# A planned attention and expert kernel: the planner gets another model of the DMA queue and new ranks, a third buffer for the probabilities, and a second load of one expert's weights

## The chip, the core and the metric

The kernel runs on one core of one Trainium2 chip. The metric is device time in microseconds (us). TensorE is PE in the profile (its weight loads are PEld), VectorE is DVE, ScalarE is ACT, GpSimd is POOL. SyncE's queue (SPq) issues every DMA of this kernel.

## What is computed

There are 8 batches of 512 tokens of 256 features, a context of 512 x 512 per batch, and a mask over the context. First cross attention with 8 heads of 32, then a layer with a shared expert and 16 routed experts:

```python
    x = x + _L0_xattn_ref(ctx_2048, _layernorm(x, axis=-1), mask_BxS2_fk1, mask_BxS2_fk1, W_src, b_src, W_tgt, b_tgt, W_out, b_out)
    x = x + _L0_ffn_ref(_layernorm(x, axis=-1), gate_w, w_gate, w_up, w_down, sw_gate, sw_up, sw_down)
```

Attention projects the context to keys and values and the normalised x to queries, masks them, takes a softmax over 512 context positions per head, multiplies by the values, and projects [tgt, update] with W_out. The second layer normalises x again, computes 16 gate scores per token, keeps the top 8 as weights, and adds the weighted sum of all 16 experts (silu(x Wg) * (x Wu)) Wd (H = 128) to a shared expert of the same form.

## The kernel before

**Split numbers.** Each float32 operand of a large matmul is held as two float16 tiles, high part and rest, and each product is three matmuls (`mm3`, line 461).

**A recorded program, then a plan.** `record` (line 433) writes down every operation as an `Op` with its engine, a modelled duration in ns and its buffers. `schedule` (line 340) then plays these operations through a model of the five queues and fixes the order in which each engine gets them; the kernel issues them in that order, all from line 1071, which is why the profile shows one line. Engines run in order, so an instruction that waits holds all behind it. Among the operations that could start first the planner takes the one with the lowest due time, `vt`: a number in batches that `record` sets by hand, plus a correction from the table `RANK` (line 202) by kind of operation and stage (start, batch 0, batch 1, the last, the rest). `AHEAD` (line 201) says how far in due time an operation may run before the oldest one that is still open. `SLOTS` (line 30) gives the number of buffers of each pool; an operation that needs a buffer waits for a free slot.

**The DMA queue in the model.** A plain DMA (`dma`, line 197) takes 360 ns of SP's time, a transposing DMA of n tiles (`dmat`, line 194) takes max(1240, 16.4 n) ns. After that, line 413 lets a transfer start 900 ns later or when the one before it is done, and lasts size/250 ns, where a transposing DMA has size 4000 n.

**Start.** x, the attention weights and the context of batch 0 are loaded. The weights are scaled by powers of two (`spread` takes a maximum over partitions with two small matmuls, `ama` and `amb`; `power` makes the scale), transposed on PE (`wsT`, `wtT`, `woT`) and split. The context of batch 0 is masked on POOL, its row sums of squares (`junk`, ACT; then `csT` and `csB` on PE) give its scale, and it is turned on PE (`cT`); later batches are turned by DMA (`ch<-cn`). The 17 experts' raw weights (`raw`, pool W, three DMAs of 128 KB each) are squared (`sqw`, ACT or POOL) and summed (`fm`, PE) for their scale, and then turned into float16 pairs (`w`, pool W; one ACT and one DVE operation each).

**Attention of a batch.** Keys `k`, queries `q` and values `v`. Then eight units (4 groups u of head group and half, times 2 blocks of 128 tokens). One unit: `s` is 16 matmuls into the only four-bank PSUM buffer S; `nm` is the row maximum (DVE, 2.3 us); four exps `p` (ACT); then per pair of heads, two of them, a float16 copy `pn` (ACT) and its rest (POOL), a transposing DMA `pt<-pn` of 128 tiles, and 16 matmuls `o` with the values. The S buffer is free for the next unit after the four exps; a `pn` buffer after its `pt` landed. `oc` and `on` scale the result; after each half, `on` is turned by DMA (`oh<-om`; batch 0 by PE) and projected (`oo`), and the second layernorm follows: statistics, an inverse root with 13 small POOL operations (`r2h`, `r2t`), `xf`, the split `fm` and four DMAs `f<-fm`, then the gate logits `lg`.

**Experts.** For each expert matmuls `g` and `u` of the tokens, `a` (ACT tanh, DVE, POOL times the gate weight `cb`, which DMA spreads over the partitions), `u` times `a`, the split `h`, and after each group of 5, 4, 4, 4 experts the down projection `y`, added into x. The experts of batch b are worked on together with the attention of batch b+1; due times and `RANK` decide the mixture.

A unit is written below as batch, group, block: unit 2,1,0.

Of the kernel before, what the change touches and what calls it, by code (L numbers as in the profile page):

```python
# [200 lines left out]
AHEAD = 1.366  # L201
RANK = {
    "aACT": {0: 0.1537, 1: 0.0033, 2: -0.4983, 7: 0.1955},
    "aDVE": {0: 0.0254, 1: 0.2498, 2: -0.2428},
    "aPOOL": {0: -0.0113, 1: 0.6968, 2: 0.5586, 7: 0.0013},
    "amaPE": {-1: 0.2806},
    "ambPE": {-1: 0.1166},
    "bobDVE": {-1: 0.5078},
    "bobSP": {-1: -0.2061},
    "bvbDVE": {-1: 0.105},  # L210
    "cTPE": {0: 0.5508},
    "cbSP": {0: 0.2177, 2: 0.7056, 7: 0.5622},
    "cdSP": {0: 0.0041, 1: -0.029, 2: 0.2104},
    "chACT": {0: -0.6068},
    "chDVE": {0: 0.2153},
    "chSP": {1: 0.0075, 2: -0.8976, 7: -1.0876},
    "cnACT": {1: -0.6307, 2: -0.7293, 7: -0.9914},
    "cnDVE": {1: 0.0087, 2: -0.0023, 7: 0.0346},
    "colsSP": {-1: -0.0672},
    "csBPE": {2: -0.1535, 7: -0.0124},  # L220
    "csTPE": {0: -0.1204, 1: -0.0287, 2: -1.2814, 7: -0.0309},
    "ctACT": {0: 0.864, 1: 0.1003, 2: 0.7227, 7: -0.1018},
    "cxPOOL": {0: 0.6459},
    "cxSP": {-1: 0.0735, 1: 0.0526, 2: -0.9286, 7: -0.0609},
    "fACT": {0: 0.0039},
    "fDVE": {0: 1.0851},
    "fSP": {1: 0.3396, 2: -0.0242, 7: 0.4824},
    "fTPE": {0: 0.3035},
    "fmACT": {1: 0.3782, 2: -0.0974, 7: -0.0187},
    "fmDVE": {2: 0.5311, 7: -0.0959},  # L230
    "fmPE": {-1: -0.1267},
    "fmaPE": {-1: 0.1564},
    "fmbPE": {-1: -0.4319},
    "gPE": {0: 0.1235, 1: 0.207, 2: 0.1559, 7: 0.6056},
    "gTPE": {0: 0.3676, 1: 0.5965, 2: -0.1162, 7: -0.0034},
    "gsqDVE": {-1: -0.4317},
    "gw_nDVE": {-1: -0.1543},
    "gw_nSP": {-1: -2.0117},
    "gwsACT": {-1: 0.0234},
    "gwsDVE": {-1: 0.6316},  # L240
    "hACT": {0: -0.6213, 1: 0.3291, 2: -0.1853, 7: -0.0131},
    "hDVE": {0: 0.1408, 1: 0.0071, 2: -0.2515, 7: -0.0144},
    "hPOOL": {0: -0.3695, 1: 0.2141, 2: -0.0944, 7: 0.3346},
    "junkACT": {1: -0.0113, 2: -0.018, 7: 0.0007},
    "kACT": {0: 0.3565, 1: -0.9183, 2: -0.1216},
    "kDVE": {0: 0.4038, 1: 0.1818, 2: -0.0333, 7: 0.0991},
    "kPE": {0: -0.2174, 1: -0.0614, 2: -0.0344, 7: -1.3012},
    "lgPE": {0: 0.2761, 1: -0.3919, 2: -0.2135, 7: 0.0154},
    "mbSP": {-1: -0.7576, 1: 0.96, 2: 0.035, 7: 0.1462},
    "mcolDVE": {-1: -0.5544},  # L250
    "mkSP": {-1: -0.0456},
    "mkTPE": {-1: -0.2494},
    "mrDVE": {0: 0.88, 1: 0.1094, 2: 0.5668},
    "mvDVE": {0: 0.3115, 1: 0.2223, 2: 0.1576, 7: -0.6709},
    "mwDVE": {1: -0.5933, 2: 0.5831, 7: -0.1328},
    "nmACT": {0: 0.3158, 1: -0.251, 2: -0.0551, 7: -0.0427},
    "nmDVE": {0: 0.0026, 1: 0.0593, 2: -0.1259, 7: -0.1155},
    "oPE": {0: 0.0273, 1: -0.0232, 2: 0.0553, 7: 0.0423},
    "oTPE": {0: 0.1833},
    "ocACT": {0: 0.1024, 1: 0.1925, 2: 0.2005, 7: 0.4061},  # L260
    "ocDVE": {0: 0.1704, 1: -0.1219, 2: -0.6326, 7: -0.0917},
    "ohACT": {0: 0.4072},
    "ohDVE": {0: -0.1733},
    "ohSP": {1: 0.1129, 2: -0.0398, 7: -0.3174},
    "omACT": {2: 0.2922, 7: 0.0002},
    "omPOOL": {1: -0.0603, 2: -0.0508, 7: 0.7467},
    "onPOOL": {0: 0.7499, 1: -0.853, 2: -0.1829, 7: -0.2491},
    "onesPOOL": {-1: -0.3119},
    "ooPE": {0: 0.4931, 1: -0.4365, 2: -0.6844, 7: -0.4352},
    "outSP": {0: 0.4027, 1: -0.3028, 2: 0.4122, 7: 0.4538},  # L270
    "pACT": {0: 0.0182, 1: -0.6748, 2: -0.0234},
    "pnACT": {0: 0.2152, 1: 0.2561, 2: 0.1906, 7: 0.0196},
    "pnPOOL": {0: 0.1635, 1: 0.0141, 2: 0.2234},
    "ptSP": {0: 0.4655, 1: -0.4384, 2: 0.1266, 7: 0.3368},
    "qACT": {0: 0.1257, 1: -0.3375, 2: -0.3996, 7: -0.129},
    "qDVE": {0: -0.2704, 1: -0.4202, 2: -0.5367, 7: -0.2649},
    "qPE": {0: -0.3731, 1: -0.0506, 2: -0.194, 7: -1.1345},
    "qPOOL": {0: -0.0185, 1: 0.126, 7: -0.8731},
    "rDVE": {0: -0.1233, 1: -0.1058, 2: 0.0001, 7: -0.3334},
    "rawSP": {-1: -0.1474},  # L280
    "rhPOOL": {0: -0.1646, 1: -0.4627, 2: 0.6826, 7: 0.2987},
    "riDVE": {0: -0.198, 1: 0.6361, 2: 0.1284, 7: -0.0834},
    "sPE": {1: 0.0314, 2: -0.3686, 7: -0.8384},
    "scACT": {0: -0.0831, 1: 0.4518, 2: -0.1934, 7: -0.1498},
    "scDVE": {0: 0.3459, 1: -0.1583, 2: 0.1869, 7: -0.186},
    "scPOOL": {0: -0.0709, 1: 0.1093, 2: -0.1766, 7: 0.0205},
    "smallDVE": {-1: 0.3026, 1: -0.1537, 2: -0.254, 7: -0.5587},
    "smallPOOL": {-1: -0.2347, 0: -0.1282, 1: -0.3163, 2: 0.0089, 7: 0.0576},
    "sqwACT": {-1: -0.5218},
    "sqwPOOL": {-1: -0.1816},  # L290
    "tDVE": {0: 0.0006, 1: -0.5031, 2: 0.36, 7: 0.0922},
    "uDVE": {0: 0.1229, 1: 0.634, 2: -0.239, 7: -0.259},
    "uPE": {0: -0.1486, 1: 0.6035, 2: 0.715},
    "vACT": {0: 0.2058, 1: 0.1873, 2: -0.0086, 7: 0.1161},
    "vDVE": {0: 0.3577, 1: 0.1322, 2: -0.9791, 7: -0.0565},
    "vPE": {0: 1.1408, 1: -1.3367, 2: -0.1245, 7: 0.2457},
    "vPOOL": {0: -0.0824, 1: -0.3013, 2: -0.4353, 7: 0.59},
    "veDVE": {0: 0.124, 1: -0.0703, 2: -0.0253, 7: -1.3962},
    "vfDVE": {0: 0.0546, 1: -0.7051, 2: 0.0069, 7: 0.2438},
    "wACT": {-1: -0.1553},  # L300
    "wDVE": {-1: -0.0168},
    "wmaPE": {-1: -0.2382},
    "wmbPE": {-1: -0.7302},
    "woACT": {-1: -0.6539},
    "woDVE": {-1: 0.1164},
    "woTPE": {-1: 0.5609},
    "wo_nSP": {-1: 0.2082},
    "wsACT": {-1: -0.3273},
    "wsDVE": {-1: -0.0925},
    "wsTPE": {-1: 0.9299},  # L310
    "ws_naSP": {-1: -0.9149},
    "ws_nbSP": {-1: 0.0231},
    "wtACT": {-1: 0.4585},
    "wtDVE": {-1: 0.4299},
    "wtTPE": {-1: -0.4778},
    "wt_nSP": {-1: 0.0823},
    "xDVE": {0: 0.124, 1: 0.2257, 2: -0.3319, 7: 0.1379},
    "xPOOL": {0: -0.0121, 1: 0.02, 2: 0.1123, 7: -0.199},
    "xSP": {0: 1.1008, 1: 0.0058, 2: 0.0641, 7: 0.353},
    "xTPE": {0: 0.4516},  # L320
    "xfACT": {0: -0.1806, 1: 0.1451, 2: -0.1422, 7: -0.437},
    "xhDVE": {0: 0.6081},
    "xhSP": {1: 0.2024, 2: -0.7682, 7: 0.2589},
    "xmACT": {1: 0.1813, 2: 0.1954},
    "xmPOOL": {1: -0.0234, 2: 0.0256, 7: 0.0077},
    "xnACT": {0: 0.0363, 1: -0.1228, 2: 0.2161, 7: -0.0338},
    "xnSP": {-1: -4.4201, 1: -0.3353, 2: -0.0611, 7: -0.0009},
    "xoPE": {0: -0.2204, 1: -0.0378, 2: -0.3262, 7: -0.1335},
    "yPE": {0: 0.3541, 2: 0.148, 7: 0.1762},
# [772 lines left out]
```

## Time and profile before

| | us |
|---|---|
| median of 3 runs | 962.2 (960.25 to 963.15) |
| the profiled execution, its own time | 962.42 |
| its span on the core | 960.3 |
| PE busy (matmuls) | 860.6, 8007 instructions |
| DVE, ACT, POOL busy | 668.5, 654.2, 680.4 |
| DMA packets' time, share of 16 engines | 77.9% on the queue of all DMAs |
| mean granted TensorE clock | 0.972 |

Busy times of an engine do not overlap with themselves; what is missing to the span is the engine's idle time. Where an engine is the bound, its idle time is the price, and the list of waits says what ended it. The windows show busy us per engine between two moments, counted from the span's start, and behind each its number of instructions.

### The profile page before, as it was taken

Reading aid. Unit: us, or ns where it says so; the run is one execution under the profiler, and the core shown is the slowest. Engines: PE = TensorE matmul, PEld = TensorE weight load, DVE = VectorE, ACT = ScalarE, POOL = GpSimd, SP = SyncE. Lnnn points to the kernel's source line nnn. Section 1 sums busy time; section 2 is a strip of 40 time slices with the busy share of each in tenths; the row PEclk is TensorE's granted clock in tenths of the full one; section 3 lists DMA queues with packets and bytes.
Section 4 is the critical chain, followed back from the end, with each engine's and each line's share of the span. In section 5 each row is a group of like instructions: output and inputs, shape, how many; then the busy total and the mean of one; then the engine's idle time right before and its main releaser. Section 6 shows DMA issues by size and latency. Waiting matters only on the chain.

```text
span 960.3 us, 21139 instructions
## 1 busy us (share of the span) xinstructions
PE 860.6 (90%) x8007; PEld 547.0 (57%) x8007; DVE 668.5 (70%) x1311; ACT 654.2 (68%) x1133; POOL 680.4 (71%) x830
## 2 busy tenths in 40 slices
PE   3874768989789998989999999989999999999997
PEld 2452446766555565636655556646555666565655
DVE  6666778855876677757785688757886687567554
ACT  3588887874877687757786587757787777534231
POOL 4577778876768787677858786787848976853432
PEclk9886999999889999999999999999999999999999
DMA  8868787798699967999599977998499968951411
GB/s 254 271 124 175 138 157 130 151 197 162 121 205 184 201 133 139 211 191 178 104 198 182 197 145 137 204 191 181 88 189 197 178 110 144 214 120 26 123 56 44
DMA packets 395542, 152.43 MB, mean 159 GB/s; under 512 B 347008, under 2 KB 375216, under 8 KB 395440
## 3 DMA queue, kind: packets, MB, share of 16 engines
q1 hardware_dynamic: 395440, 151.08, 77.9%
q8 instruction: 63, 1.03, 0.5%
q14 instruction: 39, 0.32, 0.2%
HBM read 61.12 MB, written 4.46 MB: 68 GB/s over the span
## 4 chain that ended last, share of the span: by engine, by line
PE 55%; DMA 12%; ACT 11%; DVE 8%; POOL 5%; issue 3%; SPq 1%; POOLq 0%; ACTq 0%; DVEq 0%
PE y L1071 14%; PE u L1071 13%; PE g L1071 12%; DMA pt<-pn 8%; PE s L1071 4%; ACT p L1071 3%; PE o L1071 3%; POOL pn L1071 3%; PE v L1071 3%; DVE nm L1071 3%; PE k L1071 2%; ACT pn L1071 2%; DMA cb<-cd 2%; PE oo L1071 2%; SPq L1071 1%
## 5 line engine op out<-in xcount | busy, mean ns | idle before, releaser
L1071 POOL TENSOR_TENSOR pn<-p,pn 128x1024 f16<-128x1024 f32 x128 | 274.6, 2151 | 57.8 <-ACT pn L1071 48.7
L1071 PEld LDWEIGHTS <-w 128*128 128x128 f16 x1836 | 172.1, 98 | 172.1 <-issue 19.3
L1071 POOL TENSOR_TENSOR a<-a,cb 128x512 f32<-128x512 f32 (+1 forms) x144 | 166.1, 1165 | 73.5 <-DVE a L1071 34.6
L1071 ACT ACTIVATE p<-s,nm,small 128x512 f32<-128x512 f32 x256 | 192.3, 782 | 10.6 <-POOL pn L1071 8.1
L1071 PE MATMUL g<-f,w 128*128 128x512 f16 (+1 forms) x918 | 194.7, 357 | 3.7 <-DVE oc L1071 1.3
L1071 PE MATMUL u<-f,w 128*128 128x512 f16 (+1 forms) x918 | 194.1, 358 | 1.6 <-DVE a L1071 1.6
L1071 PE MATMUL y<-w,h 128*128 128x256 f16 x1632 | 185.9, 273 | 5.6 <-DVE h L1071 4.1
L1071 PEld LDWEIGHTS <-h 128*128 128x128 f16 x1632 | 158.5, 98 | 32.0 <-DVE h L1071 6.7
L1071 ACT CAST pn<-p 128x1024 f16<-128x1024 f32 x128 | 134.5, 1053 | 60.8 <-DMA pt<-pn 60.7
L1071 DVE TENSOR_REDUCE nm<-s 128x4 f32<-128x2048 f32 x64 | 146.2, 2285 | 14.7 <-PE s L1071 14.6
L1071 ACT ACTIVATE a<-g,small 128x512 f32<-128x512 f32 (+1 forms) x153 | 98.1, 645 | 51.7 <-PE g L1071 49.8
L1071 DVE SCALAR_TENSOR_TENSOR a<-a,g 128x512 f32<-128x512 f32 (+1 forms) x153 | 94.5, 622 | 39.1 <-ACT a L1071 38.0
L1071 ACT CAST h<-u 128x512 f16<-128x512 f32 (+1 forms) x117 | 62.8, 540 | 51.0 <-DVE u L1071 49.2
L1071 PEld LDWEIGHTS <-pt 128*128 128x128 f16 x2048 | 69.8, 97 | 36.8 <-DMA pt<-pn 16.5
L1071 DVE TENSOR_TENSOR h<-u,h 128x512 f16<-128x512 f32 (+1 forms) x117 | 72.6, 625 | 25.7 <-ACT h L1071 24.1
L1071 DVE SCALAR_TENSOR_TENSOR x<-y,small,x 128x512 f32<-128x512 f32 x64 | 47.8, 748 | 60.9 <-PE y L1071 60.6
L1071 DVE TENSOR_TENSOR u<-u,a 128x512 f32<-128x512 f32 (+1 forms) x108 | 68.4, 635 | 27.5 <-PE u L1071 22.7
L1071 PE MATMUL o<-v,pt 128*128 128x65 f16 (+1 forms) x2048 | 74.2, 187 | 13.5 <-DMA pt<-pn 10.9
L1071 PE MATMUL s<-k,q 32*128 32x512 f16 x768 | 56.1, 396 | 21.2 <-ACT p L1071 20.7
L1071 POOL TENSOR_TENSOR on<-oc,r 128x128 f32<-128x128 f32 x64 | 30.1, 472 | 31.9 <-DVE oc L1071 20.1
L1071 POOL TENSOR_TENSOR h<-a,h 128x512 f16<-128x512 f32 (+1 forms) x36 | 40.3, 1120 | 15.2 <-ACT h L1071 14.9
L1071 PE MATMUL k<-ch,ws 128*128 128x512 f16 x192 | 45.6, 390 | 5.4 <-DMA ch<-cn 4.1
(188 smaller groups left out, 1055.8 us busy)
## 6 DMA issues: line engine op xcount, KB each, us to landing
cb<-cd SPq DMA_DIRECT2D x112, 256.0 KB, 3.9
cx<-in_ctx_dram SPq DMA_DIRECT2D x32, 256.0 KB, 3.6
xn<-in_x_dram SPq DMA_DIRECT2D x16, 256.0 KB, 3.4
x<-in_x_dram SPq DMA_DIRECT2D x8, 512.0 KB, 4.3
cb<-cd SPq DMA_DIRECT2D x32, 128.0 KB, 3.5
out_dram<-x SPq DMA_DIRECT2D x16, 256.0 KB, 3.1
mb<-in_mask_BxS_fk_dram SPq DMA_DIRECT2D x8, 256.0 KB, 4.6
raw<-in_L_ffn_w_gate_dram SPq DMA_DIRECT2D x16, 128.0 KB, 3.3
```

The costliest lines, as they stand in the source:

```text
L1071: getattr(getattr(nc, eng), m)(*[real(v) for v in (*out, *args_)], **{k: real(v) for k, v in kw.items()})
```

## The change

The program that `record` writes is the same but for three more DMAs. What changes:

- The model of the DMA queue. A transposing DMA of n tiles now has size 6555 n at 272 bytes per ns, starts 650 - 4.7 n ns after its issue or when the queue is free, and holds SP until 900 ns before its end; a plain DMA starts 950 ns after its issue.
- `AHEAD` and all of `RANK`, so the order on every engine.
- Buffers: `pn` 2 to 3, `oc` 2 to 3, `act` 5 to 6; `row` 2 to 1, `oh` 2 to 1, `W` 18 to 17. `gsq` moves from pool `row` to pool `act`.
- The raw weights of the last expert (15) are loaded into a slot of pool `pn` instead of W, given up after the squares, and loaded again into a `pn` slot before their conversion.

```diff
-    x=2, n2=5, cx=4, c16=2, ch=1, xh=1, f=2, qk=4, row=2, mb=1, mx=2, mt=1, p32=2, pn=2, pp=3, v3=2, oc=2, oh=2,
-    cb=3, act=5, hx=6, W=NE + 1, cd=2, mr=1,
+    x=2, n2=5, cx=4, c16=2, ch=1, xh=1, f=2, qk=4, row=1, mb=1, mx=2, mt=1, p32=2, pn=3, pp=3, v3=2, oc=3, oh=1,
+    cb=3, act=6, hx=6, W=NE, cd=2, mr=1,
...
-    def add(self, eng, dur, calls, port=False, size=0, after=()):
+    def add(self, eng, dur, calls, port=False, size=0, after=(), lead=950.0):
...
+        op.lead = lead
...
     def dmat(self, tiles, out, in_):
-        self.add("SP", max(1240.0, 16.4 * tiles), [self.call("sync.dma_start_transpose", out, in_)], size=4000 * tiles)
+        self.add("SP", max(1240.0, 16.4 * tiles), [self.call("sync.dma_start_transpose", out, in_)], size=6555 * tiles, lead=650.0 - 4.7 * tiles)
...
-AHEAD = 1.366
+AHEAD = 1.37664868967
 RANK = {
-    "aACT": {0: 0.1537, 1: 0.0033, 2: -0.4983, 7: 0.1955},
...
+    "aACT": {0: -0.467, 1: -0.4329, 2: 0.0775},
...
         if e == "SP":
-            dma_free = max(dma_free, op.end + 900.0) + op.size / 250.0
+            dma_free = max(dma_free, st + op.lead) + op.size / 272.0
             op.end = dma_free
+            if op.lead < 950.0:
+                free[e] = max(free[e], dma_free - 900.0)
...
-    gsq = Buf("row", [P, D], F32, "gsq")
+    gsq = Buf("act", [P, D], F32, "gsq")
...
+    def load_raw(e, pool):
         sg, su, sd = (io["w_gate"][e], io["w_up"][e], io["w_down"][e]) if e < E else (io["sw_gate"], io["sw_up"], io["sw_down"])
-        raw = raws[e] = Buf("W", [P, 768], F32, f"raw{e}")
+        raw = Buf(pool, [P, 768], F32, f"raw{e}{pool}")
...
+        return raw
+
+    for n, e in enumerate(order):
+        p.vt = -1.9 + 0.001 * n
+        raw = raws[e] = load_raw(e, "W" if n + 1 < NE else "pn")
...
         raw = raws.pop(e)
+        if n + 1 == NE:
+            p.vt -= 0.1
+            raw = load_raw(e, "pn")
+            p.vt += 0.1
```

More of the change, by code (lines that the diff above doesn't have):

```diff
@@ L194, in dmat @@
     def dmat(self, tiles, out, in_):
-        self.add("SP", max(1240.0, 16.4 * tiles), [self.call("sync.dma_start_transpose", out, in_)], size=4000 * tiles)
+        self.add("SP", max(1240.0, 16.4 * tiles), [self.call("sync.dma_start_transpose", out, in_)], size=6555 * tiles, lead=650.0 - 4.7 * tiles)
     def dma(self, size, out, in_):
         self.add("SP", 360.0, [self.call("sync.dma_start", out, in_)], size=size)
-AHEAD = 1.366
+AHEAD = 1.37664868967
 RANK = {
-    "aACT": {0: 0.1537, 1: 0.0033, 2: -0.4983, 7: 0.1955},
[L204 to L329, printed above, removed]
@@ new lines @@
+    "aACT": {0: -0.467, 1: -0.4329, 2: 0.0775},
+    "aDVE": {0: -0.4757, 1: -0.1412, 2: 0.1784, 7: 0.0231},
+    "aPOOL": {0: 0.0084, 1: 0.0236, 2: -0.0609, 7: -0.0052},
+    "amaPE": {-1: 0.1657},
+    "ambPE": {-1: -1.0849},
+    "bobDVE": {-1: 0.0026},
+    "bobSP": {-1: 0.0674},
+    "bvbDVE": {-1: 0.3624},
+    "cTPE": {0: 0.2135},
+    "cbSP": {0: -0.1949, 1: -0.164, 2: 0.0166, 7: -0.0706},
+    "cdSP": {0: 0.206, 1: 0.2555, 2: 0.4037, 7: 0.2962},
+    "chACT": {0: -0.0519},
+    "chDVE": {0: 0.367},
@@ new lines @@
+    "chSP": {1: -0.0463, 2: -0.2063, 7: -0.3196},
+    "cnACT": {1: -0.4583, 2: -0.0899, 7: -0.0037},
+    "cnDVE": {1: -0.4549, 2: -0.313, 7: -0.2229},
+    "colsSP": {-1: -0.5585},
+    "csBPE": {0: -0.0414, 1: 0.1005, 2: 0.0098},
+    "csTPE": {0: 0.3845, 1: -0.0799, 2: -0.0702, 7: 0.3664},
+    "ctACT": {0: 0.7724, 1: 0.3374, 2: -0.1036, 7: -0.0194},
+    "cxPOOL": {0: 0.0738},
+    "cxSP": {-1: 0.4025, 1: 0.5996, 2: -0.2329, 7: -0.0331},
+    "fACT": {0: 0.4352},
+    "fDVE": {0: -0.0913},
@@ new lines @@
+    "fSP": {1: 0.3124, 2: -0.1162, 7: 0.3436},
+    "fTPE": {0: 0.817},
+    "fmACT": {1: 0.3599, 2: -0.3531, 7: -0.6697},
+    "fmDVE": {1: 0.0777, 2: -0.0832, 7: 0.1838},
+    "fmPE": {-1: 0.0124},
+    "fmaPE": {-1: -0.1525},
+    "fmbPE": {-1: 0.3713},
+    "gPE": {0: -0.0025, 1: 0.0372, 2: -0.007, 7: 0.0964},
+    "gTPE": {0: 0.5506, 1: 0.0428, 2: -0.0004, 7: -0.2184},
+    "gsqDVE": {-1: 0.2967},
+    "gw_nDVE": {-1: -0.4048},
+    "gw_nSP": {-1: -0.5034},
+    "gwsDVE": {-1: 0.0828},
+    "hACT": {0: -0.6742, 1: 0.1845, 2: -0.3722, 7: -0.0007},
@@ new lines @@
+    "hDVE": {0: 0.1928, 1: -0.1416, 2: -0.2732, 7: 0.4049},
+    "hPOOL": {0: -0.0127, 1: 0.0298, 2: 0.1888, 7: 0.8},
+    "junkACT": {0: 0.4516, 1: -0.327, 2: -0.0551, 7: -0.0895},
+    "kACT": {0: 0.4062, 1: -0.0091, 2: 0.3583, 7: 0.4622},
+    "kDVE": {0: -0.3335, 1: -0.0114, 2: -0.3475, 7: -0.6756},
+    "kPE": {0: 0.4216, 1: 0.2242, 2: -0.02, 7: 0.0272},
+    "lgPE": {0: 0.154, 1: -0.0204, 2: -0.2155, 7: 0.0139},
+    "mbSP": {-1: 1.0822, 1: 0.8488, 2: -0.0648, 7: -0.0484},
+    "mcolDVE": {-1: -0.0043},
@@ new lines @@
+    "mkSP": {-1: -0.4686},
+    "mkTPE": {-1: 0.2334},
+    "mrDVE": {0: 0.6552, 1: -0.0009, 2: -0.302, 7: 0.053},
+    "mvDVE": {1: -0.1573, 2: 0.1491, 7: -0.1027},
+    "mwDVE": {0: -0.1171, 1: 0.2834, 2: -0.0153, 7: 0.5712},
+    "nmACT": {0: 0.5742, 1: -0.2397, 2: 0.2178, 7: -0.1795},
+    "nmDVE": {0: 0.0826, 1: 0.3058, 2: 0.2106, 7: -0.0512},
+    "oPE": {0: 0.1872, 1: 0.1546, 2: -0.0387, 7: -0.1254},
+    "oTPE": {0: 0.2165},
+    "ocACT": {0: 0.5143, 1: 0.5347, 2: 0.1003, 7: -0.2753},
+    "ocDVE": {0: 0.1521, 1: 0.0406, 2: 0.0368, 7: 0.0417},
@@ new lines @@
+    "ohACT": {0: -0.0205},
+    "ohDVE": {0: 0.1997},
+    "ohSP": {1: -0.1054, 2: -0.1686, 7: -0.8489},
+    "omACT": {1: -0.2925, 2: -0.5016, 7: 0.403},
+    "omPOOL": {1: -0.1555, 2: -0.0724, 7: 0.4818},
+    "onPOOL": {0: -0.0007, 2: 0.0987, 7: -0.0131},
+    "onesPOOL": {-1: 0.199},
+    "ooPE": {0: -0.1661, 1: -0.057, 2: -0.1361, 7: -0.1256},
+    "outSP": {0: 0.0322, 1: -0.0126, 2: -0.1168},
+    "pACT": {0: -0.1925, 1: 0.1274, 2: 0.0025, 7: -0.0488},
+    "pnACT": {0: -0.2814, 2: -0.3285, 7: 0.189},
@@ new lines @@
+    "pnPOOL": {0: -0.0188, 1: 0.0673, 2: 0.0362, 7: -0.3038},
+    "psbPE": {-1: 0.7063},
+    "psgwPE": {-1: -0.0554},
+    "ptSP": {0: 0.0228, 1: 0.4216, 2: 0.0986, 7: -0.0892},
+    "qACT": {0: -0.1236, 1: -0.0223, 2: -0.2262, 7: -0.1551},
+    "qDVE": {0: 0.2501, 1: -0.3393, 2: -0.1701, 7: -0.0182},
+    "qPE": {0: -0.1996, 1: -0.0652, 2: -0.0215, 7: 0.0497},
+    "qPOOL": {0: 0.2946, 1: 0.4058, 2: 0.0164, 7: 0.2389},
+    "rDVE": {1: 0.2673, 2: 0.0826, 7: -0.0608},
+    "rawpnSP": {-1: 0.506},
@@ new lines @@
+    "rhPOOL": {0: -0.077, 1: 0.6315, 7: -0.554},
+    "riDVE": {0: -0.0942, 1: -0.0956, 2: 0.0021, 7: -0.4101},
+    "sPE": {0: 0.4941, 1: -0.0509, 2: -0.5668, 7: -0.504},
+    "scACT": {0: -0.0566, 1: -0.0112, 2: 0.2103, 7: -0.1885},
+    "scDVE": {0: 0.2056, 1: 0.0706, 2: -0.0556, 7: 0.5249},
+    "scPOOL": {0: -0.0343, 1: 0.2354, 2: -0.2508, 7: 0.0989},
+    "selDVE": {-1: 0.0065},
+    "smallDVE": {-1: -0.1137, 0: 0.4597, 1: -0.0784, 2: 0.0195, 7: -0.4726},
+    "smallPOOL": {-1: 0.6575, 0: 0.003, 1: -0.1854, 2: 0.0339, 7: -0.4249},
@@ new lines @@
+    "sqwACT": {-1: -0.4909},
+    "sqwPOOL": {-1: 0.1285},
+    "tDVE": {0: -0.016, 1: 0.0355, 2: -0.3012, 7: -0.0231},
+    "uDVE": {0: 0.2387, 1: -0.0303, 2: -0.0139, 7: 0.6204},
+    "uPE": {0: 0.0429, 1: 0.4079, 2: 0.1012, 7: -0.027},
+    "vACT": {0: 0.1635, 1: -0.0474, 2: -0.6005, 7: 0.1675},
+    "vDVE": {0: 0.1743, 1: -0.4829, 2: -0.9168, 7: 0.3204},
+    "vPE": {0: 0.0003, 1: -0.1638, 2: -0.0191, 7: 0.1022},
+    "vPOOL": {0: 0.0065, 1: -0.1163, 2: -0.4408, 7: 0.1077},
+    "veDVE": {0: 0.2356, 1: -0.028, 2: 0.3229, 7: 0.0008},
@@ new lines @@
+    "vfDVE": {0: 0.0511, 1: -0.077, 2: 0.0626, 7: -0.1077},
+    "wACT": {-1: -0.5424},
+    "wmaPE": {-1: 0.2232},
+    "wmbPE": {-1: -0.576},
+    "woACT": {-1: 0.7086},
+    "woDVE": {-1: 0.02},
+    "woTPE": {-1: 0.5711},
+    "wo_nSP": {-1: 0.2314},
+    "wsACT": {-1: 0.7085},
+    "wsDVE": {-1: -0.0012},
+    "wsTPE": {-1: -0.2614},
+    "ws_naSP": {-1: -0.832},
+    "ws_nbSP": {-1: -0.7734},
+    "wtACT": {-1: -0.3959},
+    "wtDVE": {-1: -0.1396},
+    "wtTPE": {-1: -0.2564},
+    "wt_nSP": {-1: -3.2959},
@@ new lines @@
+    "xDVE": {0: 0.068, 1: 0.1906, 2: -0.3593, 7: 0.2863},
+    "xPOOL": {0: -0.0286, 1: 0.0215, 2: -0.4895, 7: -0.0052},
+    "xSP": {0: 0.1849, 1: -0.0423, 2: -0.0372, 7: 0.0805},
+    "xTPE": {0: 0.0463},
+    "xfACT": {0: -0.0421, 1: -0.4738, 2: -0.0772, 7: -0.8138},
+    "xhACT": {0: -0.1113},
+    "xhDVE": {0: -0.3523},
+    "xhSP": {1: -0.0747, 7: 0.1156},
+    "xmACT": {1: -1.1798, 2: 0.0085, 7: 0.0904},
+    "xmPOOL": {1: -0.0081, 2: -0.3909, 7: -0.8113},
+    "xnACT": {0: 0.4575, 1: -0.0277, 2: 0.3466, 7: -0.0321},
@@ L330 @@
+    "xnSP": {-1: -0.1983, 1: -0.2358, 2: -0.1322, 7: 0.0196},
+    "xoPE": {0: -0.638, 1: 0.0832, 2: -0.0315, 7: 0.2598},
+    "yPE": {0: 0.1496, 1: -0.0891, 2: 0.0016, 7: 0.0802},
 }
@@ L651, in record @@
     raws, sqs = {}, []
-    for n, e in enumerate(order):
-        p.vt = -1.9 + 0.001 * n
+    def load_raw(e, pool):
         sg, su, sd = (io["w_gate"][e], io["w_up"][e], io["w_down"][e]) if e < E else (io["sw_gate"], io["sw_up"], io["sw_down"])
-        raw = raws[e] = Buf("W", [P, 768], F32, f"raw{e}")
+        raw = Buf(pool, [P, 768], F32, f"raw{e}{pool}")
         r4 = raw[:, 0:512].rearrange("p (k j h) -> p k j h", k=2, j=2)
```

## The prediction

> **What bounds the kernel now.** I read the engine totals first, then the busy time by windows, then the waits of each window, then single tiles. PE is the fullest engine:
>
> ```profile
> span 960.3 us, 21139 instructions
> PE 860.6 (90%) x8007; PEld 547.0 (57%) x8007; DVE 668.5 (70%) x1311; ACT 654.2 (68%) x1133; POOL 680.4 (71%) x830
> ```
>
> The change adds no matmul and takes none away, so what it can move is the 99.7 us in which PE stands idle (960.3 - 860.6). The windows show where they lie (us; PE, PEld, DVE, ACT, POOL busy with counts; granted clock; DMA share; GB/s):
>
> ```profile
> 0.00:36.00 36.00, 18.44 (x76) 12.05 (x77) 24.47 (x88) 14.45 (x27) 14.30 (x44) 0.95 0.88 258
> 36.00:135.00 99.00, 66.03 (x776) 43.20 (x775) 65.68 (x129) 84.05 (x141) 75.23 (x87) 0.86 0.77 160
> 135.00:250.00 115.00, 102.95 (x1129) 79.65 (x1127) 85.79 (x196) 86.43 (x172) 90.39 (x125) 0.97 0.85 159
> 250.00:850.00 600.00, 567.83 (x5349) 347.09 (x5350) 427.94 (x788) 433.94 (x736) 458.51 (x527) 0.99 0.87 170
> 850.00:960.00 110.00, 105.37 (x687) 65.03 (x684) 64.62 (x113) 35.33 (x60) 42.00 (x52) 1.00 0.24 67
> ```
>
> Window length less PE's busy time gives idle of 17.6, 33.0, 12.1, 32.2 and 4.6 us. So almost two thirds of it lies in the first quarter, where batch 0 has no experts' work to mix in. There ACT is 85% busy (84.05 of 99), and PE's longest wait from 36 to 135 is for its exps, which free the only score buffer:
>
> ```profile
> PE s L1071 <- ACT p L1071: 16.7, 5, 7.0
> ```
>
> From 250 to 850 it is the transposing DMA. First ACT, which waits for a `pn` buffer to be read out, then PE, which waits for the result:
>
> ```profile
> ACT pn L1071 <- DMA pt<-pn: 59.2, 33, 6.4
> PE o L1071 <- DMA pt<-pn: 10.3, 8, 3.1
> ```
>
> ACT's 59.2 us cost nothing by themselves, but all that is queued behind `pn` on ACT stands too. From 36 to 135 that same wait is 0.7 us: a third buffer gives nothing there.
>
> **Does the new queue model fit the trace?** The tile view of `pt` (issue on SP in ns, min/median/max; then issue to landing):
>
> ```profile
> L1071 SPq DMA_TRANSPOSE pt<-pn x128: 1316/2576/5387, 53.0 to 840.0; - x128
> DMA to landing us min/median/max: 4.2/4.7/8.2
> ```
>
> By the code, the old plan let a `pt` land for its readers at 2.10 + 0.90 + 2.05 + 1.20 = 6.25 us, but let the queue go after 2.05. The new one says 0.05 + 3.08 + 1.20 = 4.33 us and holds the queue for 3.08. The shortest landing is 4.2; two `pt` issued together held SP for 4.52 to 6.72 us from 480 to 590, 3 us each. The new model is the nearer in both, so its order should be upset less by the real queue. [...]
>
> **Method.** I gave each instruction of the trace its place in the program, engine by engine, and added up the busy time that stands ahead of a landmark in the old order and in the new one, both with the durations of this trace. The time of a landmark can only be bounded so, not told.
>
> **A, up to the first score block** (old: 39.9 us). PE has 22.4 us of work ahead of it, in the new order 30.7: the values and more transposes come first. Now PE starts late, since `wt_n` is the 14th DMA and `ama` waits for its maximum until 14.3. In the new order `wt_n` and W_src are the first five DMAs, and `ama` needs only `mkT` (9.1 now) and those: 5 to 6 us earlier. Against that, `csT` to `csB` takes 7.0 us (19.7 to 26.7), with 6.2 us of PE work between; the new order has 0.4. Then 23.6 us of work follow. I put the new block at about 43.5: idle 12.8 against 17.5, **-4** (ends -6, and +2 if the 7.0 us stay and nothing is early).
>
> **B, from there to the last score block of batch 1** (197.8). Between the first exp of batch 0 (44.2) and the last group of batch 1 (213.6) ACT has 141.8 us of work in 169.4, 84%. In the new order it is 140.4, with PE's share of the stretch 0.9 less. The weights' conversions move from batch 0 to batch 1 (ACT between first and last group of batch 0: 64.1 down to 54.7), and 14.5 us of PE work leave the gaps of batch 0 too, so each half alone says little. At 84% the stretch is 167.7, at 89% (the best slice now, 21.4 of 24 us from 96 to 120) 157.7, at 80% 175.5; with the 0.9 that is -1 to -11, and +7. DMA is no tighter: the new order has 87 us of service between first and last `pt` of batch 1 where the old has 90, which really took some 77. I take a pace of 87%: **-6**.
>
> **C, from batch 2 on.** PE's waits that a DMA ends there are 10.3 (`o`), 3.9 (`lg<-f`), 1.6 (`k<-ch`), 1.2 (`oo<-oh`), and 2.5 and 1.4 (`k`, `q`) just before 250: 20.9 us. For `o` I added for each of the 96 pairs of batches 2 to 7 the chain that can't be shorter: 2.25 (`nm`), what stands on ACT from the first exp to this `pn`, 2.13 (POOL), 4.3 (DMA), 0.65 of hand-overs. Against PE's work between `s` and `o` it is too long for 2 pairs (2.3 us in all) now, and for 4 (2.3 us too) in the new order; the work on ACT falls from 6.8 to 5.3 us a pair, and the median slack rises from 9.2 to 10.6. So 8 of the 10.3 come from queues, and these the third buffer and the model address. I take 8 there and 4 of the other 10.6: **-12** (ends 0 and -21).
>
> **D, the gate logits.** This is the price. Between `oo` of a batch's second half and `lg` PE now has 13.8 (batch 1), 25.2, 29.2, 29.2, 30.5, 25.3, 22.1 us of work (batch 7); in the new order 10.5, 19.2, 18.8, 17.9, 16.2, 18.3, 13.0. The chain from batch 7's rows: `x`, statistics and roots 7.9, four `xf` 2.06, two `fm` copies 1.24, DVE 0.68, two DMAs to landing 3.7: 15.6. By that batch 7 loses 2.6 and batch 1 no more than now. Now the last `f` lands 20.4 to 31.6 us after `oo`, since nothing hurries it. At 20.4 the loss is 7.4 + 11.7 (batches 2 to 6) + 3.7 (batch 1) = 23. I take the chain's rows, **+4** (0 to +23).
>
> **Small things.** The three more DMAs are some 1.3 us of queue at 0.4 each (`raw` rows, one behind the other), in a stretch where DMA is 77 to 85% busy: 0 to +1.3, taken as 0. `raw15` holds one `pn` slot from the reload to its conversion, so batch 0's last unit and batch 1's first two still have two buffers. One `row` and one `oh` fewer: a `q32` lives some 2.5 us (0.75 + 0.62 + 1.16), and in the new order more PE work lies between two of them; 0. Clock: in the windows up to 135 it is 0.95 and 0.86; 14.5 us of PE work leave the slow one, worth 14.5 x 0.14 = **-2** (0 if the gaps there, which grow, lower it further). [...]
>
> **Sum.** -4 - 6 - 12 + 4 - 2 = -20 us: span 940.3, and with the 2.1 us around it **942.4** (the profiled execution, 962.42, is 0.2 from the median).
>
> **Rivals.**
> - *Gains given back.* ACT keeps its 84%, so B is -1; C brings 4 of 21; A, D as above, no clock: -5, about 957. For it: ACT, POOL and DMA are all at 75 to 85% from 36 to 250, and the third buffer isn't there for batch 0's first two units. This is also the case that the change doesn't do what it says. 11%.
> - *All of it.* A -6, B -11, C -19, D 0, clock -2: -38, 924. For it: the model fits both rows of `pt`. 12%.
> - *Slower: PE waits for the gate logits.* If the chain from `oo` to `lg` stays as long as the shortest now, D costs 23, and C nothing as its `f` are in that chain's queue: -4 - 6 + 0 + 23 = +13, 975. With C at nothing it decides from a chain of about 18 us on, where D passes 10. For it: its latency followed the cover in every batch so far; against it, the new order has the four `xf` and both `fm` of batch 7 side by side on ACT. 17%.
>
> **Numbers.** Forecast (932 to 954) 60%. Within 0.3% of the time before, 2.9 us, is about what a measurement of this kernel can't tell from no change. Of the first rival 7 of 11 fall within it, the rest is faster: faster 0.76, same 0.07, slower 0.17. The range leaves out the fastest ends and most of the slower rival: 924 to 967.
>
> **What would show it.** PE idle by the same windows: about 13 to the first score block (near 43), the 16.7 of `s<-p` at 12 or less; from 250 to 850 `ACT pn <- DMA pt` well under 59.2 and `PE o <- DMA pt` near 2; `PE lg <- DMA f` at 4 to 8, none of batches 2 to 6. ACT busy in 36 to 214 says which pace B had. I am wrong if the last score block of batch 1 starts later than 200 without more PE work done, or if `lg` waits in each batch.

## The result, and the profile after

The kernel after takes 990.4 us (median of 6 runs, 988.2 to 994.2) where the kernel before, beside it, takes 961.8 (960.3 to 963.2): a ratio of 1.0304, 95% interval 1.0279 to 1.0329. It is 28.5 us slower; 942.4 was forecast, and the range ended at 967.

The first lines of the page of the kernel after, against 960.3 and 860.6 before:

```profile
span 987.7 us, 21128 instructions
...
PE 872.0 (88%) x8007; PEld 556.4 (56%) x8007; DVE 681.4 (69%) x1311; ACT 654.3 (66%) x1133; POOL 674.6 (68%) x830
```

The span grew by 27.4 us: PE's idle time by 16.0 (99.7 to 115.7) and its busy time by 11.4, for the same 8007 matmuls. The windows, with the same columns as those of before, say where:

```profile
0.00:36.00 36.00, 19.86 (x116) 16.30 (x117) 24.75 (x90) 14.57 (x29) 14.36 (x45) 0.86 0.85 248
36.00:135.00 99.00, 63.48 (x690) 40.65 (x689) 63.38 (x118) 74.88 (x126) 68.61 (x82) 0.74 0.75 159
135.00:250.00 115.00, 102.31 (x1119) 78.08 (x1117) 91.37 (x188) 89.07 (x179) 87.73 (x118) 0.99 0.82 155
250.00:850.00 600.00, 557.12 (x5142) 340.93 (x5140) 423.15 (x777) 423.22 (x714) 436.62 (x517) 0.97 0.80 161
850.00:988.00 138.00, 129.20 (x950) 80.39 (x948) 78.71 (x141) 52.60 (x89) 67.32 (x72) 1.00 0.40 97
```

Idle in them is 16.1, 35.5, 12.7, 42.9 and 8.8 us, against 17.6, 33.0, 12.1, 32.2 and 4.6: the idle time grew where the forecast had it shrink, from 250 us on, by 14.9. And the granted clock fell: 0.95 to 0.86, 0.86 to 0.74, and 0.99 to 0.97 from 250 to 850 (from 135 to 250 it rose, 0.97 to 0.99). The records behind that column hold two values only in these two traces, 1.0 and 0.5. In the trace of before PE worked 38.8 us at 0.5, in that of after 71.5. Half of it is my estimate of what the full clock would have saved (a score block took 1.89 us at 0.5 and 1.04 at 1.0): 19.4 and 35.8 us, called **clock cost** below. What is left of the span without idle and clock cost is 841.2 and 836.2, the matmuls themselves. So the 27.4 are 16.0 of idle and 16.4 of clock, less 5.0.

The waits from 250 to 850, first ACT's, then PE's:

```profile
ACT nm L1085 <- DVE nm L1085: 59.1, 26, 5.3
...
ACT pn L1085 <- DMA pt<-pn: 6.6, 3, 4.4
```

```profile
PE csB L1085 <- DVE small L1085: 10.1, 4, 3.2
PE s L1085 <- ACT p L1085: 9.3, 10, 1.8
PE o L1085 <- DMA pt<-pn: 5.3, 4, 2.3
PE lg L1085 <- DMA f<-fm: 4.1, 4, 2.3
PE v L1085 <- DMA ch<-cn: 4.0, 1, 4.0
```

Three of the same rows in the kernel before:

```profile
ACT nm L1071 <- DVE nm L1071: 24.6, 25, 2.6
```

```profile
PE csB L1071 <- DVE small L1071: 3.0, 2, 2.8
...
PE s L1071 <- ACT p L1071: 1.3, 1, 1.3
```

ACT's wait for a `pn` buffer fell from 59.2 to 6.6 us as the third buffer promised, and its wait for the row maxima rose from 24.6 to 59.1: most of the same idle time behind another name. PE's wait for `pt` halved (10.3 to 5.3), and new short waits stand beside it: `csB` 10.1 (3.0 before), `s` 9.3 (1.3), `v` 4.0. None is over 4.0 us.

### The profile page after: what moved, and what is told of

The parts are those of the page before. It is cut to its first block, busy times and chain, and to the rows that moved or that the text cites. A ratio compares the mean times of both kernels' runs of the same rounds, so it can differ in the third digit from the quotient of the medians.

```text
span 987.7 us, 21128 instructions
## 1 busy us (share of the span) xinstructions
PE 872.0 (88%) x8007; PEld 556.4 (56%) x8007; DVE 681.4 (69%) x1311; ACT 654.3 (66%) x1133; POOL 674.6 (68%) x830
## 4 chain that ended last, share of the span: by engine, by line
PE 55%; DVE 10%; ACT 9%; DMA 8%; POOL 6%; issue 4%; SPq 1%; DVEq 0%; POOLq 0%; ACTq 0%
PE y L1085 16%; PE g L1085 13%; PE u L1085 12%; PE s L1085 4%; DMA pt<-pn 3%; PE o L1085 3%; ACT p L1085 3%; POOL pn L1085 2%; DVE nm L1085 2%; PE v L1085 2%; PE k L1085 2%; PE oo L1085 2%; DVE small L1085 2%; ACT pn L1085 1%; POOL a L1085 1%
## 5 line engine op out<-in xcount | busy, mean ns | idle before, releaser
L1085 PEld LDWEIGHTS <-w 128*128 128x128 f16 x1836 | 174.4, 98 | 175.0 <-issue 25.7
L1085 PE MATMUL g<-f,w 128*128 128x512 f16 (+1 forms) x918 | 201.7, 364 | 5.0 <-DVE k L1085 1.8
L1085 ACT ACTIVATE p<-s,nm,small 128x512 f32<-128x512 f32 x256 | 190.1, 781 | 17.5 <-POOL pn L1085 14.4
L1085 PE MATMUL y<-w,h 128*128 128x256 f16 x1632 | 191.5, 277 | 4.3 <-DVE h L1085 4.2
L1085 PEld LDWEIGHTS <-h 128*128 128x128 f16 x1632 | 160.6, 99 | 35.0 <-DVE h L1085 5.3
L1085 DVE TENSOR_REDUCE nm<-s 128x4 f32<-128x2048 f32 x64 | 146.2, 2284 | 23.3 <-PE s L1085 22.9
L1085 ACT ACTIVATE a<-g,small 128x512 f32<-128x512 f32 (+1 forms) x153 | 97.8, 644 | 50.2 <-PE g L1085 49.7
L1085 ACT CAST h<-u 128x512 f16<-128x512 f32 (+1 forms) x117 | 62.7, 539 | 53.5 <-DVE u L1085 53.1
L1085 PEld LDWEIGHTS <-pt 128*128 128x128 f16 x2048 | 72.4, 98 | 39.8 <-DMA pt<-pn 18.2
L1085 PE MATMUL o<-v,pt 128*128 128x65 f16 (+1 forms) x2048 | 77.1, 188 | 15.1 <-DMA pt<-pn 13.0
L1085 PE MATMUL s<-k,q 32*128 32x512 f16 x768 | 58.0, 403 | 26.7 <-ACT p L1085 20.8
L1085 ACT ACTIVATE nm<-nm,small 128x4 f32<-128x4 f32 x64 | 24.9, 389 | 72.6 <-DVE nm L1085 72.4
L1085 POOL TENSOR_TENSOR h<-a,h 128x512 f16<-128x512 f32 (+1 forms) x36 | 38.7, 1076 | 24.5 <-ACT h L1085 24.5
L1085 PE MATMUL v<-ws,ch 128*128 128x256 f16 x384 | 47.3, 283 | 4.0 <-DMA ch<-cn 4.0
```

Of the source, the lines that this page charges most:

```text
L1085: getattr(getattr(nc, eng), m)(*[real(v) for v in (*out, *args_)], **{k: real(v) for k, v in kw.items()})
```

## The experiments

Two words are used in them. A **written-out order** is a kernel whose program is issued in a fixed list instead of being planned at build time; so an order can be kept while buffers change, or be planned with other settings:

```diff
+ORDER = """
...
-    ops = schedule(record(io))
+    ops = fixed_order(record(io))
```

The **planned end** is the time at which the planner's own model ends. It is no measurement; it is given because the planner chooses by it. It is 925.0 for the kernel before (by the old queue model, with 20.5 us of PE idle from 250 us to the end) and 950.3 for the kernel after (new model, 45.5). The two are measured by two models, so they don't compare as they stand. Theories at the start: the order loses the time; or the buffers and the second load do; and, within the order, the clock's answer to short gaps or the waits themselves.

### 1. The old order with the new buffers

The order of the kernel before on every engine, with `pn` 3, `oh` 1, `W` 17 and the last weights loaded twice (`row` 2, `act` 5, `oc` 2 as before).

> The old order exactly, on every engine, written out as a list and not planned again; with the third buffer for the probabilities, one oh buffer instead of two, 17 weight slots, and the last expert's raw weights loaded a second time. Theory (the loss of the kernel after is in its new order: more short gaps of PE, which the granted clock doubles; the buffers help by themselves): 945 to 962 us, ACT's wait of pn for the transposing DMA under 20 us (59.2 before), PE's wait of o for pt at 5 or less (10.3), half-clock time about 56 us as before. Rival (the buffers and the second load cost the time, for instance the one oh buffer or three more transfers in the full stretch of the DMA): 975 us or more, with waits for oh or raw that the kernel before doesn't have.

Measured: 961.4 us, ratio 0.9996 (0.9971 to 1.0021). ACT's and PE's waits for `pt` and ACT's for the maxima, from 250 to 850:

```profile
ACT nm L1224 <- DVE nm L1224: 34.7, 28, 4.1
...
ACT pn L1224 <- DMA pt<-pn: 11.4, 4, 4.3
```

```profile
PE o L1224 <- DMA pt<-pn: 8.1, 6, 3.5
```

These buffers and the second load cost nothing, so the loss lies in the order or in the buffers that this run left as they were (experiment 11 has those too). The third buffer takes 48 us of ACT's waiting away and 2.2 of PE's, whose wait stays at 8.1 where I expected 5 or less. Idle fell by 7.4 us (92.3), and the clock cost rose by 10.0 (29.4) in this execution: the time stood still.

### 2. Unused matmuls in the gaps

The kernel after with matmuls of 512 columns, their results unused, ahead of seven waiting PE instructions. They add some 0.22 us each to PE's busy time, 15.8 us in all.

```diff
+WARM = {"csT1": 6, "o001": 8, "csB3": 12, "v30": 14, "csB4": 11, "o401": 8, "csB5": 13}
```

> The kernel after with unused matmuls of 128x128 put ahead of seven PE instructions that wait (csT of batch 1, o of unit 0,0,0, csB of 3, 4 and 5, v of 3, o of unit 4,0,0), 72 in all; the order and the rest are unchanged. They keep PE busy in gaps of 2.1 to 4.3 us, so that the clock has no reason to fall. Theory (the gaps cost twice, once as idle and once by the half clock that follows; PE worked 71.5 us at half clock, before 38.8): time at half clock falls from 105 us to 60 to 85, total 978 to 986. Rival (the granted clock falls for another reason and only the idle counts): 987 to 996, time at half clock 95 us or more.

Measured: 988.7 us, ratio 1.0269 (1.0244 to 1.0294). The clock did answer. The windows around `csB` of batches 4 and 5, first of the kernel after, then of this one (the same work, some us earlier):

```profile
381.00:392.00 11.00, 9.36 (x92) 7.11 (x96) 8.66 (x24) 5.49 (x9) 4.47 (x10) 0.84 0.90 164
484.00:496.00 12.00, 7.65 (x59) 4.90 (x60) 7.80 (x21) 6.65 (x11) 5.41 (x7) 0.57 0.79 132
```

```profile
380.00:391.00 11.00, 10.69 (x107) 7.20 (x104) 9.81 (x27) 5.83 (x11) 5.50 (x10) 1.00 0.92 188
478.00:491.00 13.00, 11.50 (x131) 6.69 (x130) 12.01 (x32) 9.41 (x19) 8.55 (x12) 1.00 0.65 126
```

0.84 and 0.57 became 1.00, so PE's idle time there is what halves it. But in all the clock cost fell by 5.3 only (35.8 to 30.5; other half-clock stretches came up, at 297 and 908 us), and the time by 1.7, too little to be told from noise. PE's idle time and the unused matmuls together are 120.4 us (104.6 + 15.8), where the kernel after has 115.7 idle: PE waited 4.7 us more. Both theories were half right; filling gaps is no cure.

### 3. and 4. Half of the one order, half of the other

Written-out orders with all buffers of the kernel after, joined behind the experts of batch 0 (about 250 us).

> The old order up to the end of batch 0's experts (about 250 us), then the new order; all buffers of the kernel after. It asks where in the order the loss arises. By the landmarks, corrected for the work of PE done by then, the kernel after has lost 8 us by that point and 20 us behind it. Theory (the loss arises all along, most of it in the steady batches): 976 to 986 us. Rival (the loss is the early stretch's, and what follows is only carried on): 955 to 968.

> The new order up to the end of batch 0's experts (about 250 us), then the old order; all buffers of the kernel after. Theory (the loss arises all along, 8 us early and 20 behind): 962 to 974 us. Rival (the loss is the early stretch's): 982 to 992.

Measured: old then new 988.4 us, 1.0271 (1.0238 to 1.0304); new then old 983.7, 1.0213 (1.0187 to 1.0238). The late part of the new order costs most of it by itself: 26 us, of which 3 were lost by 250 (from there on idle is 48.9 and clock cost 17.9, against 37.1 and 5.8 in the kernel before). The second missed its range and fell in its rival's: it has one gap of 12.1 us at 265, at the seam, that neither kernel has. Counted at the same pieces of work, and with the work of PE done by then taken out, it had lost 9 us at 250, 8 more at the seam, and 4 behind it. So the early part costs some 9 us, the late part about 20, as the kernel after has it (7 to 8, and 20).

### 5. The queue by itself

Behind the end of experiment 1: 8 transposing DMAs that wait for each other, then 24 in a row, three buffers in turn.

```diff
+    for k in range(8):
+        turn(0, 0)
+    for k in range(24):
+        turn(k % 3, k % len(pns))
```

> The kernel of the old order with the new buffers, and behind its end two rows of transposing DMAs of 128 tiles between buffers that are free then, their results unused: first 8, each of which waits for the landing of the one before it, then 24 with up to three in the queue. New queue model: 4.3 us for each of the 8 and 3.08 us for each of the 24. Old queue model: 6.25 us for each of the 8 and 2.05 to 2.1 us for each of the 24. Theory (a lone transfer is as the new model has it, a queued one is nearer to the old one): 4.3 us and 2.1 to 2.6 us.

The tile view of `pt` in the two stretches (issue on SP in ns, then issue to landing in us):

```profile
L1234 SPq DMA_TRANSPOSE pt<-pn x8: 1317/1854/2307, 955.3 to 985.5; - x8
...
DMA to landing us min/median/max: 4.2/4.3/4.6
```

```profile
L1234 SPq DMA_TRANSPOSE pt<-pn x24: 1780/2339/3034, 989.8 to 1046.9; - x24
...
DMA to landing us min/median/max: 4.3/4.8/5.2
```

A lone one lands after 4.3 us, as the new model says. In a row, with nothing else in the queue, one lands every 2.48 us ((1046.9 - 989.8) / 23 between issues): the new model's 3.08 is too slow, the old one's 2.05 too fast. For the 524 KB of a `pt` that is 211 GB/s in this run, where the two models have 170 and 256: the measurement stands between the old model and the one that I preferred to it.

### 6. to 9. Other queue models, from the new ranks

From here on orders are planned anew by the kernel's planner, its ranks moved by a search (100,000 small random changes, kept where the planned end falls), and written out. They have program and buffers of the kernel after (`gw_n`, one small buffer of the start, in pool `act`). The mixed model lets a queued transfer take a share of its time:

```diff
-            dma_free = max(dma_free, st + op.lead) + op.size / 272.0
+            x = op.size / 272.0
+            dma_free = max(dma_free + (0.68 if op.lead < 950.0 else 0.8) * x, st + op.lead + x)
```

> The program and buffers of the kernel after, with the order planned by the same planner and the same new queue model, but with ranks from a longer search (100,000 small random changes of the ranks, kept where the planned end falls; it ends at 947.5 us by the planner's model, where the kernel after has 950.3). Theory (the queue model is too slow for queued transfers, and no rank can mend an order that is planned for a DMA bound which isn't there): 978 to 992 us, PE idle behind 250 us at 45 or more. Rival (the ranks of the kernel after are merely badly chosen): under 972.

> As the run with the new queue model, with the same start, steps and durations, but in the planner's queue a transposing transfer that stands behind another takes 0.68 of the new model's time (2.1 us for 128 tiles) and a plain one 0.8; a lone one lands as in the new model. The planned end is 926.0 us. Theory (queue model): 952 to 968 us, PE idle behind 250 us under 40. Rival (any order that is planned with such short landings is upset on the chip): 975 or more.

> As the run with the mixed queue model, and the planner also has the median durations of each kind of operation from the trace of the kernel before, and counts each PE gap over 1 us as 0.5 us more, for the clock. Theory (an order planned with what the trace shows beats both kernels): 942 to 957 us. Rival (the gaps that the plan can't see, from DVE waiting for POOL and from the clock, take it back): 958 or more.

> Program and buffers of the kernel after, planned with the old queue model, from the same start and with the same search as the two runs with the new and the mixed queue model; planned end 930.3 us. Three orders planned with three queue models are then to be compared, searched alike. Theory A (what is lost lies in the queue model, and the old one is the best of the three): 955 to 968 us. Theory B (an order that is fitted to the planner's model alone comes out near 985 whatever its queue model, and the order of the kernel before is better than its plan for a reason the plan does not hold): 976 to 992.

Measured: new model 982.5 us, 1.0203 (1.0155 to 1.0252); mixed 984.5, 1.0241 (1.0197 to 1.0284); measured durations 990.7, 1.0308 (1.0272 to 1.0344); old model 983.1, 1.0243 (1.0218 to 1.0267). My theory of the queue model fell: three models, one time. Of the four, the plan with the best knowledge took the longest. Theory B, that a plan's end by its own model doesn't tell the time, was left.

### 10. The kernel before, planned anew

Only its ranks and `AHEAD` are changed: the ranks moved by a random 0.02, then both searched.

> The kernel before with nothing changed but its ranks: all of them moved by a random 0.02, and then searched again (100,000 small changes) with its own old queue model, to a planned end of 922.5 us, which is 2.5 us earlier than that of the kernel before. Theory A (the planned end under the old queue model tells the time): 955 to 966 us. Theory B (fitted to the plan alone, an order loses its margins on the chip): 976 to 992 us, with more short waits of PE for DVE, ACT and DMA than before, and more time at half clock.

Measured: 958.3 us, 0.9978 (0.9953 to 1.0003). Theory B falls too, as a general rule: another order of the old kind keeps the time. So the start of the search, the buffers, or both with the queue model had to be told apart.

### 11. to 16. From the old ranks

The same search, started from the ranks of the kernel before (moved a little at random in 11, 14 and 16).

> Program, buffers and queue model of the kernel after; only the ranks are others: the search started from the ranks of the kernel before (moved by a random 0.01, since they stand still as they are) and not from the new ones. Planned end 927.8 us, where the kernel after has 950.3 and the same search from its own ranks 947.5. Theory C (neither the queue model nor the buffers lose the time; the new ranks are a poor fit even to their own model, and the search can't leave them): 952 to 966 us. Rival (the new queue model or the buffers lose it): 976 to 992.

> Program and buffers of the kernel after, the old queue model, and the search started from the ranks of the kernel before. Planned end 932.4 us; the run with the old model from the new ranks had 930.3 and took 983. Theory C (the start of the ranks decides, the planned end says little between starts): 954 to 968 us. Rival (the buffers of the kernel after cost about 20 us when an order is planned for them): 976 to 990.

> The buffers of the run with the old order (row 2, act 5, oc 2), planned from the ranks of the kernel before with the median durations of the trace, the queue as the run of the queue alone measured it (a queued transfer takes 0.8 of the new model's time), and 0.5 us of price more for each PE gap over 1 us by the clock's cost. Planned end 908.8 us by these durations; the order of the kernel before has 937 in the same replay and takes 960. Theory C: 935 to 955 us, faster than both kernels. Rival (a plan this tight loses on the chip what it has no margin for, as the measured plan from the new ranks did): 960 to 990.

Measured: new model 957.1 us, ratio 0.9922 (0.9893 to 0.9950), faster than both kernels, by 0.8% against the one before; old model 982.4, 1.0201 (1.0133 to 1.0269); measured durations 990.1, 1.0269 (1.0197 to 1.0342). The first clears the queue model and the buffers of the change: with both, and other ranks, the loss is gone. The third was a miss too and came out as its rival had it. The second was a miss of theory C, and gave theory D: with three `pn` buffers more transfers can stand in the queue, and a plan that takes the queue too fast is hurt by it.

> As the run with the new model from the old ranks (three pn buffers), with another seed of the search. Planned end 927.8 us. Theory D (with three pn buffers, up to three transfers stand in the queue, and a plan must take its queue as slow as the new model does): 950 to 966 us. Rival (orders scatter): anything up to 990, with no relation to the model.

> As the run with the old model from the old ranks (three pn buffers), with another seed of the search. Planned end 928.7 us. Theory D: 974 to 990 us, with PE waits behind 250 us for transfers that stand behind pt (xh, ch, oh, f) or for pt itself, above those of the new model's orders. Rival (orders scatter): 955 to 966.

> As the run before, but planned with two pn buffers, as the kernel before has; the other buffers and the second load of the last weights as in the kernel after. Planned end 926.1 us. Theory D (the buffers limit the queue there, so the old model does no harm): 952 to 968 us. Rival (the other buffers or the scatter of orders): 974 to 990.

Measured: new model again 958.3 us, 0.9953 (0.9933 to 0.9973); old model again 975.1, 1.0118 (1.0067 to 1.0168); old model with two `pn` buffers 953.7, 0.9890 (0.9844 to 0.9936), the fastest of all. All three fell where theory D had them. PE's waits for DMAs from 250 to 850 in the first run with the old model and three buffers, in the second, and in the new model's second:

```profile
PE q L1227 <- DMA xh<-xm: 11.4, 4, 4.2
...
PE o L1227 <- DMA pt<-pn: 1.7, 3, 0.6
```

```profile
PE o L1227 <- DMA pt<-pn: 12.6, 8, 3.3
...
PE oo L1227 <- DMA oh<-om: 4.6, 4, 1.5
```

```profile
PE o L1227 <- DMA pt<-pn: 6.3, 7, 2.7
```

With the old model something small stands behind the `pt` in each: once `xh`, once `oh` and `pt` itself. That these waits are the mechanism of theory D is argued; that three buffers and the old model go badly together, twice, and well with two, is measured. Both plans with measured durations (experiments 8 and 13) also took the queue faster than the new model does.

### All orders side by side

The planned end is by each order's own planner, with PE's planned idle from 250 us to the end in brackets (a dash where it isn't known). One ruler is the end of the same fixed order by one and the same planner, that of the kernel after, with the queue as experiment 5 measured it: a queued transfer takes 0.8 of the new model's time. Time is the median; idle and clock cost are of the profiled execution (which in 6 had a span of 988.4, above the median).

| | ranks from | queue model, `pn` | planned end (idle from 250 on) | one ruler | time | idle (from 250 on) | clock cost |
|---|---|---|---|---|---|---|---|
| before | old | old, 2 | 925.0 (20.5) | 926.1 | 961.8 | 99.7 (37.1) | 19.4 |
| 10 | old | old, 2 | 922.5 (17.7) | 923.7 | 958.3 | 97.8 (29.3) | 25.1 |
| 16 | old | old, 2 | 926.1 (21.2) | 923.6 | 953.7 | 90.4 (25.7) | 23.7 |
| 12 | old | old, 3 | 932.4 (27.4) | 933.1 | 982.4 | 110.4 (41.4) | 26.1 |
| 15 | old | old, 3 | 928.7 (23.9) | 930.4 | 975.1 | 107.2 (41.2) | 24.1 |
| 11 | old | new, 3 | 927.8 (24.5) | 926.0 | 957.1 | 92.0 (28.7) | 16.6 |
| 14 | old | new, 3 | 927.8 (24.5) | 925.4 | 958.3 | 92.4 (27.6) | 20.8 |
| after | new | new, 3 | 950.3 (45.5) | 949.0 | 990.4 | 115.7 (51.4) | 35.8 |
| 6 | new | new, 3 | 947.5 (42.8) | 946.2 | 982.5 | 111.4 (51.0) | 35.7 |
| 9 | new | old, 3 | 930.3 (27.5) | 927.6 | 983.1 | 111.5 (39.8) | 29.2 |
| 7 | new | mixed, 3 | 926.0 (21.8) | 932.8 | 984.5 | 113.3 (44.9) | 28.6 |
| 8 | new | mixed, measured, 3 | - | 948.1 | 990.7 | 117.0 (53.1) | 27.9 |
| 13 | old | measured, 3 | 908.8 (-) | 941.9 | 990.1 | 118.6 (47.4) | 28.3 |

The four rows of the new model with three buffers answer the question. Its plans are kept: 3 to 8 us more idle from 250 us on than planned, in each (16.6 more in the kernel before). But the ranks of the change leave 45.5 us of idle there in their own plan, and ranks from the old ones 24.5 under the same model and buffers. Most of the loss of the kernel after was in its plan.

The one ruler says the same of all orders, and more than their own planners do. All that end by 926.1 on it took 954 to 962 us, experiment 1 (926.1) included; all that end at 927.6 or later took 975 to 991, experiments 3 (959.7) and 4 (942.0) included. The kernel after ends 22.9 us later than the kernel before, of the 28.5 measured. By the new queue model it is the other way round: there the old order ends at 957.8, 7.5 us after the new one, so that model chose the wrong order. The border is narrow, the ranking within each side isn't right, and no order was planned to this ruler with the planner's own durations, so as a way to plan it is untested.

The same windows of experiment 11, where PE is busy 576.5 of the 600 us that it has 557.1 of in the kernel after:

```profile
36.00:135.00 99.00, 67.24 (x723) 42.91 (x722) 66.43 (x121) 80.27 (x128) 66.20 (x77) 0.78 0.75 163
135.00:250.00 115.00, 103.15 (x1157) 80.59 (x1157) 85.99 (x200) 90.34 (x177) 90.42 (x122) 1.00 0.83 159
250.00:850.00 600.00, 576.46 (x5430) 354.73 (x5429) 443.40 (x802) 443.15 (x748) 464.02 (x539) 0.99 0.89 172
```

## Why the prediction was wrong, point by point

The step that failed is the one from a truer queue model to a faster order. It put the idle time that the new order holds by itself at nothing; the plan has 45.5 us of it from 250 us on, and the run 51.4, where the old order's run has 37.1. In the sum, C was to bring 12 us and PE's idle time there grew by 14.9; the clock was to bring 2 and cost 16.4.

- **"The new model is the nearer in both, so its order should be upset less by the real queue."** Here the forecast turned to the wrong side. The sentence holds: the run has 5.9 us more idle from 250 on than planned, the kernel before 16.6. What I drew from it doesn't: an order that is upset less isn't a better order, and I never looked for the idle time that the order holds by itself. Adding up the busy time ahead of a landmark, as I did for A, B and D, shows work that is moved and no gap. The reading of the row was also only half right: "3 us each" for two `pt` issued together was SP's time, which holds other waits too; in a row they land every 2.48 us.
- **A, to the first score block, -4.** Right in time, and in part by luck: it starts at 43.9 us (43.5 forecast). `ama` did start 5.1 us earlier (14.3 to 9.2), and `csT` to `csB` takes 3.7 us. But PE is idle for 16.5 us ahead of it, not 12.8, and its work took 27.4, not the 30.7 that I carried over from the old trace. (My own figures, 12.8 against 17.5, make -5.)
- **B, batches 0 and 1, -6.** Wrong, and the sign that I named came: the last score block of batch 1 starts at 214.6, not before 200. PE has 147.4 us of work ahead of it there by the durations of before, against 140.1, so 9.4 us are lost by then (214.6 - 147.4 less 197.8 - 140.1). ACT is busy 142.0 us of the 178.1 from its first exp to the last group, 80%, the slow end of what I had weighed; and at my 87% the working gives -7, not -6. The wait that I named did shrink (`s` for the exps, 36 to 135: 16.7 to 9.5), but `o` for `pt` (6.6), `s` for `oh` (4.3) and `csT` (3.4) came up beside it. Idle from 36 to 250 grew by 3.1 only; the clock cost up to that landmark by 8.8. A score block of batch 0 takes 1.9 us at half clock and 1.04 at full, and the exps wait for it.
- **C, from batch 2 on, -12.** The mechanism was there (59.2 to 6.6 on ACT, 10.3 to 5.3 on PE), and its worth was mis-sized: 5 us of `o`, 2.2 of them under the old order, and nothing of the time in experiment 1. Most of ACT's waiting moved to the maxima. Idle from 250 on grew by 14.9 where I had it shrink by 12.
- **D, the gate logits, +4.** Their wait is 4.1 us after 3.9 from 250 to 850, and not in each batch: the cover that shrank was still enough. The rival built on it didn't happen; its time, 975, lay nearer for another reason.
- **Clock, -2.** The largest miss of a single term: +16.4. I priced the work that leaves a slow stretch, and left it at "0 if the gaps grow". The gaps grew in number, from 26 over 1.1 us to 32, and behind many of them the clock is at 0.5 for 3.4 to 24 us. The kernel before had a row that spoke for the 0: from 72 to 96, with two gaps of 7.0 us, its clock is 0.64. The length of a gap alone didn't tell what followed: at 382.6 a gap of 2.8 us ended and 3.4 us at half clock came, and 10.2 us at half clock began at 485 with gaps of 2.3 and 3.2 us, while gaps of 3.0 and 3.1 us in the kernel before (at 372 and 420) were followed by none. The 16.4 belong to one pair of executions: the one of the kernel before has a mean granted clock of 0.972, where thirteen others beside experiment 1 have 0.957 to 0.970 and the six of the kernel after 0.941 to 0.950.
- **Small things, 0.** Held: the second load and the fewer buffers cost nothing (experiments 1 and 11).

No case of mine had the idle time of the order itself as the mechanism of a loss. What stays open: which ranks of the change make its plan so much worse than the 927.8 that its model allows; how much of the 28.5 us is the clock's and how much idle time, beyond the one pair of executions; by what waits a plan with a fast queue loses 20 us with three `pn` buffers; and why a plan with measured durations is the worst kept (13: 908.8 planned, 990.1 measured).

## What to carry to other kernels

A planned order has idle time of its own; read it from the plan before asking whether the plan's model is true, compare it with what the same model can reach from another start, and compare two orders by one model and never each by its own. A wait that vanishes from an engine off the bound is no gain: look for the next wait on that engine (here 53 us left `pn` and 35 came up at `nm`). Short gaps of PE may have to be priced twice, once as idle and once by the half clock behind them (here 2.8 us up to 382.6, then 3.4 us at half clock), and a queue model is to be judged by a lone transfer and by a row of them, since the two needn't fit one line (here 4.3 us to landing, and one every 2.48 us).
